# Spectral loop of a convolution, attention and long-filter block: how its PSUM banks, copies and products are arranged

## The chip, the cores and the metric

One core of one Trainium2 chip runs the whole program. The metric is the device time of one execution in microseconds (us). The engines are TensorE (PE, with its weight loads PEld), VectorE (DVE), ScalarE (ACT), GpSimd (POOL) and SyncE (SP), which here issues most DMAs.

## The reference

The input is x of 4 x 56 x 56 x 128 floats. Layer 0 adds a 7 x 7 neighbourhood attention over group-normalised x. Layer 1 sees the image as 3136 tokens of 128 channels. It adds a linear attention, and then the part that matters here: for each of 16 filters k, a causal convolution along the tokens by FFT, followed by a 128 x 128 matrix, once for u and once for u with alternating sign, all summed:

```
U_plus = irfft(rfft(phi)[None, :, :, None] * rfft(u)[:, :, None, :])[:, :sl]
out = einsum('btkd,k,kde->bte', U_plus, s, Mpp) + einsum('btkd,k,kde->bte', U_minus, s, Mpm)
```

The sum over k and d can be taken in the frequency domain: for every frequency there is one complex 128 x 128 matrix, the filter-weighted sum of the M's, which multiplies the transformed tokens.

## The kernel before

The program has three stages. The first 1488.5 us prepare tables, run both attentions and write row transforms of the tokens to a DRAM tile `xd`. The last 154 us (L1036 on) transform columns back and add the result to the output. Between them stands the spectral loop (L881 to L1033), which the change edits. All data are fp32.

The loop runs over N1 = 42 row frequencies m1, with three more iterations to drain (LAG = 3, L1005). Each m1 has N2 = 56 column frequencies m2. One iteration `it` does four things, for different m1 at once:

- `matrices(it, gt, eh)` (L927), for eh = 0 to 7: sixteen matmuls with 32 rows each, four row groups at once, make the complex matrices of all m2 for 16 of the 128 output channels e. They go to two PSUM tiles `pg`, each of two banks: row groups 0 and 1 to the first, 2 and 3 to the second. DVE copies the first tile to `gt` and ACT the second (L941 to L946). `gt` is laid out as m2, e, real/imaginary (L1010), and pool `ps_g` has one buffer for each of the two tiles (L884).
- `token_points(it, ..., s)` (L912), for s = 0 and 1 in the turns eh = 1 and 3: four matmuls make the token transforms of one half into bank `u`; DVE copies real and imaginary parts to `us`, ACT writes the negated imaginary part (L924, L925).
- `product` (L948) for the previous m1 (ap = it - 1): for each m2, two accumulating matmuls with the 16 columns of `us` as weights and `gt[:, m2, :, c]` as moving data, an element every 8 bytes. m2 % 4 picks the column tile, so the result lies on 16 of 32 partitions of a quarter of bank `py`; 16 m2 fill one bank, and `ps_y` has two. Each turn eh does seven m2. `gather` (L961) copies a full `py` to `ys` by four instructions, one for each quarter, alternately on ACT and DVE. `regroup` (L970) sends `ys` to DRAM by four DMAs (`yd`) and fetches it back by two (`yg`).
- `columns(it - 3)` (L984) in the turn eh = 5: two back transforms, each of one matmul of 512 columns into the one bank `z`, copied by ACT (L996), then two DMAs to `zd`.

The trace shows each fp32 matmul as two MATMUL and two LDWEIGHTS records: 28 records are the 14 matmuls of seven m2.

PE's order is that of the text (`manual_schedule`, L1006). For the other engines a scheduler places instructions; in the trace DVE and ACT keep the text's order, and SP's stream in an iteration is `yg`, `xm` (tokens of a later m1, L906), `zd`, `yd`. Tables (`v`, `tok`, `back`) are fetched for six m1 at a time (L890). Semaphores come from the framework: an instruction waits for those that wrote or read the same tile. `evacuate` (L179) is a helper used elsewhere in the program: one copy, ACT and DVE by turns.

Of the kernel before, what the change touches and what calls it, by code (L numbers as in the profile page):

```python
# [10 lines left out]
F32 = mybir.dt.float32  # L11
# [4 lines left out]
P = 128  # L16
B, H, W, C = 4, 56, 56, 128
# [33 lines left out]
NS, BR = 2, H // 2  # L51
N1, N2 = 42, W
NP = N1 * N2
NG = 4
# [66 lines left out]
def hybrid_kernel(  # L121
# [759 lines left out]
    with ExitStack() as ph:  # L881
        tabs = ph.enter_context(tc.tile_pool(name="tabs", bufs=2))
        sp = ph.enter_context(tc.tile_pool(name="sp", bufs=2))
        ps_g = ph.enter_context(tc.tile_pool(name="ps_g", bufs=1, space=bass.MemoryType.PSUM))  # L884
        ps_y = ph.enter_context(tc.tile_pool(name="ps_y", bufs=2, space=bass.MemoryType.PSUM))
        ps_x = ph.enter_context(tc.tile_pool(name="ps_x", bufs=1, space=bass.MemoryType.PSUM))

        chunk = {}

        def tables_of(m1):  # L890

            c0, i = divmod(m1, CH)
            if c0 not in chunk:
                got = []
                for name, src, rows in (
                    ("v", vd, P),
                    ("tok", table["tok"], 2 * N2),
                    ("back", table["back"], 2 * N2),
                ):
                    tl = tabs.tile([rows, CH, 2 * N2], F32, tag=name, name=name)  # L900
                    nc.sync.dma_start(tl, src[:, c0 * CH : (c0 + 1) * CH])
                    got.append(tl)
                chunk[c0] = got
            return [tl[:, i] for tl in chunk[c0]]
# [6 lines left out]

        def token_points(m1, xm, us, s):  # L912

            pu = ps_x.tile([P, B, 2, N2], F32, tag="u", name="pu")
            for b in range(B):
                nc.tensor.matmul(  # L916
                    pu[:, b].rearrange("p c m -> p (c m)"),
                    xm[:, s, b, :],
                    tables_of(m1)[1],
                    start=True,  # L920
                    stop=True,
                )
            at = slice(s * B, (s + 1) * B)
            nc.vector.tensor_copy(us[:, 1:3, at, :], pu.rearrange("p b c m -> p c b m"))  # L924
            nc.scalar.mul(us[:, 0, at, :], pu[:, :, 1, :], -1.0)  # L925

        def matrices(m1, gt, eh):  # L927

            v = tables_of(m1)[0]
            pg = [ps_g.tile([P, 2, 512], F32, tag=f"g{q}", name=f"pg{q}") for q in range(2)]  # L930
            for i in range(4):
                for g in range(NG):
                    rows = slice(32 * g, 32 * (g + 1))
                    nc.tensor.matmul(  # L934
                        pg[g // 2][:, g % 2, 2 * N2 * i : 2 * N2 * (i + 1)],
                        mats[rows, 4 * eh + i, :],
                        v[rows],
                        start=True,
                        stop=True,
                    )  # L940
            for q, copy in enumerate((nc.vector.tensor_copy, nc.scalar.copy)):  # L941
                e0 = 16 * eh + 8 * q
                copy(  # L943
                    gt[:, :, e0 : e0 + 8, :].rearrange("p m (g i) c -> p g m i c", g=2),
                    pg[q][:, :, : 8 * N2].rearrange("p g (i m c) -> p g m i c", i=4, c=2),
                )  # L946

        def product(py, gt, us, m2):  # L948

            j, slot = m2 % NG, m2 // NG % 4  # L950
            for c in range(2):

                nc.tensor.matmul(  # L953
                    py[32 * j : 32 * j + 2 * NSB, slot, :],
                    us[:, 1 - c : 3 - c, :, m2],
                    gt[:, m2, :, c],
                    start=(c == 0),
                    stop=(c == 1),
                )

        def gather(py, ys, q):  # L961

            n = min(4, N2 // NG - 4 * q)
            for j in range(NG):
                rows = slice(32 * j, 32 * j + 2 * NSB)
                (nc.vector.tensor_copy if j % 2 else nc.scalar.copy)(  # L966
                    ys[rows, 4 * q : 4 * q + n], py[rows, :n]
                )

        def regroup(m1, ys):  # L970
# [10 lines left out]
                )  # L981
            return yg

        def columns(m1, yg):  # L984

            zs = sp.tile([2 * N2, NS, B * C], F32, name="zs")
            for s in range(NS):
                pz = ps_x.tile([2 * N2, B * C], F32, tag="z", name="pz")
                nc.tensor.matmul(  # L989
                    pz,  # L990
                    tables_of(m1)[2],
                    yg[:, s * B : (s + 1) * B].rearrange("p k e -> p (k e)"),
                    start=True,
                    stop=True,
                )
                nc.scalar.copy(zs[:, s], pz)  # L996
            for part in range(2):
                nc.sync.dma_start(
                    zd[:, part * N1 + m1].rearrange("w s b e -> w (s b e)"),
                    zs[part * N2 : (part + 1) * N2].rearrange("w s f -> w (s f)"),  # L1000
                )

        xms = {0: load_tokens(0)}
        gts, uss, ygs = {}, {}, {}
        LAG = 3  # L1005
        with tc.manual_schedule(engines={mybir.EngineType.PE}):  # L1006
            for it in range(N1 + LAG):
                ap = it - 1
                if it < N1:
                    gts[it] = sp.tile([P, N2, C, 2], F32, name="gt")  # L1010
                    uss[it] = sp.tile([P, 3, NSB, N2], F32, name="us")
                    if it + 1 < N1:
                        xms[it + 1] = load_tokens(it + 1)
                if 0 <= ap < N1:
                    ys = sp.tile([P, N2 // NG, C], F32, name="ys")
                done = 0
                for eh in range(8):
                    if it < N1:
                        matrices(it, gts[it], eh)
                        if eh in (1, 3):  # L1020
                            token_points(it, xms[it], uss[it], eh // 2)
                    if eh == 5 and 0 <= it - LAG < N1:
                        columns(it - LAG, ygs.pop(it - LAG))
                    if 0 <= ap < N1:
                        for m2 in range(7 * eh, 7 * eh + 7):
                            if m2 % 16 == 0:
                                py = ps_y.tile([P, 4, C], F32, name="py")
                            product(py, gts[ap], uss[ap], m2)
                            if m2 % 16 == 15 or m2 == N2 - 1:
                                gather(py, ys, m2 // 16)  # L1030
                if 0 <= ap < N1:
                    ygs[ap] = regroup(ap, ys)
                xms.pop(it, None), gts.pop(ap, None), uss.pop(ap, None)  # L1033


    with ExitStack() as ph:  # L1036
# [91 lines left out]
```

## Time and profile before

| | us |
|---|---|
| median of three runs | 2741.33 (2734.8 to 2744.59) |
| profiled execution | 2739.52 |
| its span | 2737.7 |
| stages before the loop | 0 to 1488.5, PE busy 997, granted clock 0.65 |
| spectral loop | 1488.5 to 2583.9 (1095.4), PE busy 946, PEld 740, DVE 624, ACT 542, POOL 0, clock 0.98 |
| last stage | 2583.9 to 2737.7, PE busy 126, clock 0.50, DMA share 0.82 |
| copies of `gt`: DVE, ACT | 336 each, 1.091 and 0.906 each |
| copies of `ys`: DVE, ACT | 336 each, 0.69 and 0.57 for 512 elements |

Times of one execution come from a hardware profile. A busy PE is not a PE at its peak, since matmuls are pipelined. Idle time of an engine matters only where it lies on the chain of waits that sets the end: that chain is followed back from the last instruction, at each step to what released it.

### The profile page before, as it was taken

What the parts mean: (1) busy time and instruction counts of PE and PEld (TensorE: products, weight loads), DVE (VectorE), ACT (ScalarE), POOL (GpSimd) and SP (SyncE); (2) the same over time, 40 slices, a digit from 0 to 9 for tenths busy, and PEclk for the clock granted to TensorE, in tenths of its full rate; (3) what the DMA queues carried; (4) which work ended last, traced back from release to release, by engine and by line L of the source; (5) the groups of instructions that cost most, each with busy time, mean ns of one, the idle gap of its engine ahead of it and who ended that gap; (6) DMA issues with size and microseconds to landing.
All of it is one profiled execution on the core that took longest, in us unless ns stands there. A gap on an engine that the chain in (4) does not pass through costs nothing.

```text
span 2737.7 us, 67019 instructions
## 1 busy us (share of the span) xinstructions
PE 2069.0 (76%) x28284; PEld 1419.4 (52%) x28284; DVE 1331.0 (49%) x3228; ACT 1072.3 (39%) x2521; POOL 694.2 (25%) x1227
## 2 busy tenths in 40 slices
PE   3066687666776677776686888888888888888598
PEld 3034456244563445534463767666766666676322
DVE  5244445444454443444432556555555655555232
ACT  0034433344424444244441455555555555555200
POOL 1146734376424664257630000000000000000000
PEclk7565579555885557855585899999999999999755
DMA  6620003300043000420015233333333333333497
GB/s 163 144 88 26 27 1 106 100 26 23 9 113 88 27 19 14 111 66 26 16 44 139 42 81 81 81 81 79 89 78 86 81 86 76 76 80 65 105 229 199
DMA packets 219519, 210.11 MB, mean 77 GB/s; under 512 B 43154, under 2 KB 187250, under 8 KB 218642
## 3 DMA queue, kind: packets, MB, share of 16 engines
q1 hardware_dynamic: 197850, 189.31, 27.9%
q10 hardware_dynamic: 21368, 16.51, 2.3%
q8 instruction: 222, 3.64, 0.5%
q14 instruction: 79, 0.65, 0.1%
HBM read 116.32 MB, written 89.45 MB: 75 GB/s over the span
## 4 chain that ended last, share of the span: by engine, by line
PE 42%; ACT 19%; DVE 18%; DMA 9%; issue 6%; POOL 5%; SPq 1%; ACTq 1%; DVEq 0%; POOLq 0%
ACT st L747 8%; PE pg L934 7%; DVE ys L966 7%; PE py L953 6%; PE sp L723 6%; ACT ys L966 5%; DVE gt L943 5%; PE pt L770 4%; PE bs L543 4%; ACT gt L943 3%; PE po L1059 2%; DMA xd<-xs 2%; DVE st L736 2%; PE pz L989 2%; PE pu L916 2%
## 5 line engine op out<-in xcount | busy, mean ns | idle before, releaser
L758 POOL TENSOR_SCALAR st<-st,rec 96x252 f32<-96x252 f32 (+1 forms) x560 | 484.9, 880 | 370.9 <-DVE rec L756 216.5
L943 DVE COPY gt<-pg 128x896 f32<-128x896 f32 x336 | 366.7, 1091 | 288.4 <-PE pg L934 279.1
L934 PE MATMUL pg<-v,mats 32*128 32x112 f32 x10752 | 398.9, 286 | 103.2 <-DVE gt L943 86.1
L934 PEld LDWEIGHTS pg<-v,mats 32*128 32x128 f32 x10752 | 338.5, 190 | 192.4 <-DVE gt L943 167.1
L747 ACT ACTIVATE st<-st,nmx 96x252 f32<-96x252 f32 (+1 forms) x560 | 270.4, 484 | 351.2 <-DVE nmx L736 351.2
L943 ACT COPY gt<-pg 128x896 f32<-128x896 f32 x336 | 304.4, 906 | 244.7 <-PE pg L934 233.5
L770 PE MATMUL pt<-ident,st 96*126 96x96 f32 (+1 forms) x1120 | 233.8, 360 | 214.6 <-ACT p L774 162.6
L953 PE MATMUL py<-gt,us 128*16 128x128 f32 x9408 | 389.7, 283 | 2.5 <-DVE gt L943 1.6
L770 PEld LDWEIGHTS pt<-ident,st 96*126 96x126 f32 (+1 forms) x1120 | 159.4, 207 | 347.0 <-POOL st L758 252.1
L953 PEld LDWEIGHTS py<-gt,us 128*16 128x16 f32 x9408 | 295.0, 112 | 67.4 <-issue 31.1
L966 DVE COPY ys<-py 16x512 f32<-16x512 f32 (+1 forms) x336 | 209.5, 624 | 160.2 <-ACT ys L966 157.8
L736 DVE CUSTOM_DVE_ANT_0 st<-sp,relb 96x252 f32<-96x252 f32 (+1 forms) x560 | 195.3, 400 | 87.8 <-PE sp L723 87.1
L966 ACT COPY ys<-py 16x512 f32<-16x512 f32 (+1 forms) x336 | 174.6, 520 | 149.2 <-DVE ys L966 141.1
L723 PE MATMUL sp<-kp,qT 32*96 32x252 f32 (+1 forms) x1120 | 162.2, 647 | 3.3 <-DVE xs L185 1.8
L774 DVE COPY p<-pt 126x384 f32<-126x384 f32 (+1 forms) x140 | 74.2, 530 | 160.3 <-PE pt L770 160.3
L594 ACT ACTIVATE hn<-acc,v 128x128 f32<-128x128 f32 (+1 forms) x208 | 88.1, 484 | 153.2 <-POOL v L586 138.9
L1059 PE MATMUL po<-z,onto 84*56 84x512 f32 x224 | 126.0, 1066 | 21.8 <-DMA z<-zd 21.8
L989 PE MATMUL pz<-yg,back 112*112 112x512 f32 x168 | 96.5, 657 | 46.3 <-ACT zs L996 36.2
L785 PE MATMUL po<-p,v_sb 126*32 126x96 f32 (+1 forms) x2240 | 112.6, 349 | 0.8 <-DVE aT L792 0.8
L505 PE MATMUL px<-uin,into 28*84 28x512 f32 x224 | 77.0, 960 | 36.2 <-DVE xs L185 19.7
L747 ACT ACTIVATION_READ_ACCUMULATOR st<-st,nmx 96x1 f32 (+1 forms) x560 | 104.4, 186 | 0.0
L1068 DVE SCALAR_TENSOR_TENSOR tl<-po,hmask,tl 56x512 f32<-56x512 f32 x56 | 42.0, 750 | 124.3 <-PE po L1059 123.7
(162 smaller groups left out, 2221.3 us busy)
## 6 DMA issues: line engine op xcount, KB each, us to landing
xd<-xs SPq DMA_DIRECT2D x112, 168.0 KB
xm<-xd SPq DMA_DIRECT2D x84, 224.0 KB
yd<-ys SPq DMA_DIRECT2D x168, 112.0 KB
yg<-yd SPq DMA_DIRECT2D x84, 224.0 KB
zd<-zs SPq DMA_DIRECT2D x84, 224.0 KB
z<-zd SPq DMA_DIRECT2D x14, 1344.0 KB
v_sb<-vpad SPq DMA_DIRECT2D x224, 63.0 KB
vpad<-vt SPq DMA_DIRECT2D x56, 112.0 KB
```

The lines of the kernel that those rows point to most:

```text
L723: nc.tensor.matmul(sp[h // 2][:nq, h % 2, : 2 * kn], qT[hs, ty, QR * x0 : QR * x0 + nq], kp[hs, y0 : y0 + KR, x0 : x0 + kc], start=True, s ...
L736: nc.vector.tensor_tensor_reduce(st[:nq, h, : 2 * kn], sp[h // 2][:nq, h % 2, : 2 * kn], relb[qc][:, h], -1.0, 3.0e38, ALU.add, ALU.min, n ...
L747: nc.scalar.activation(st[:nq, h, : 2 * kn], st[:nq, h, : 2 * kn], AF.Exp, bias=nmx[:nq, h : h + 1], scale=-1.0, accum_out=ssum[:nq, h : h ...
L758: nc.gpsimd.tensor_scalar(st[:nq, h, : 2 * kn], st[:nq, h, : 2 * kn], rec[:nq, h : h + 1], None, ALU.mult)
L770: nc.tensor.transpose(pt[:kn, h, :nq], st[:nq, h, c * kn : (c + 1) * kn], ident[:nq, :nq])
L785: nc.tensor.matmul(po[hs], v_sb[:kn, c, hs], pc[c][:kn, h, :nq], start=(c == 0), stop=(c == 1),)
L934: nc.tensor.matmul(pg[g // 2][:, g % 2, 2 * N2 * i : 2 * N2 * (i + 1)], mats[rows, 4 * eh + i, :], v[rows], start=True, stop=True,)
L943: copy(gt[:, :, e0 : e0 + 8, :].rearrange("p m (g i) c -> p g m i c", g=2), pg[q][:, :, : 8 * N2].rearrange("p g (i m c) -> p g m i c", i= ...
L953: nc.tensor.matmul(py[32 * j : 32 * j + 2 * NSB, slot, :], us[:, 1 - c : 3 - c, :, m2], gt[:, m2, :, c], start=(c == 0), stop=(c == 1),)
L966: (nc.vector.tensor_copy if j % 2 else nc.scalar.copy)(ys[rows, 4 * q : 4 * q + n], py[rows, :n])
L989: nc.tensor.matmul(pz, tables_of(m1)[2], yg[:, s * B : (s + 1) * B].rearrange("p k e -> p (k e)"), start=True, stop=True,)
L1059: nc.tensor.matmul(po[64 * q : 64 * q + H].rearrange("p b c -> p (b c)"), onto[:, s], zin[q][:, i, s], start=(s == 0), stop=(s == NS - 1),)
```

## The change

Only the spectral loop is edited.

- PSUM: `ps_g` has three buffers of two banks under one tag, so the two `pg` tiles of a turn take two of three in rotation. `py` has one bank (tag y), and one more bank has tag x. Token points and column transforms use bank x for s = 0 and bank y for s = 1.
- `gt` is laid out as e, m2, real/imaginary. Each `pg` tile is copied by two instructions, DVE for its first bank and ACT for its second, each to a contiguous stretch of `gt`. The moving operand of a product, `gt[:, :, m2, c]`, then has an element every 448 bytes.
- `us` has five parts in place of three, of which the last two stay zero; two such tiles are set up once by GpSimd and used by turns. The weights of a product have 32 columns, so that all 128 partitions of `py` are written (half of each quarter's rows are not used), and `evacuate` copies a `py` bank by one instruction.
- The turns eh = 0 to 6 do eight m2 each. The turn eh = 7 has no products; after its matrices it does both token points and then both column transforms. The column results are copied by `evacuate`.
- The two `zd` stores are issued after `regroup`.

```diff
@@ -881,9 +881,16 @@
     with ExitStack() as ph:
         tabs = ph.enter_context(tc.tile_pool(name="tabs", bufs=2))
         sp = ph.enter_context(tc.tile_pool(name="sp", bufs=2))
-        ps_g = ph.enter_context(tc.tile_pool(name="ps_g", bufs=1, space=bass.MemoryType.PSUM))
-        ps_y = ph.enter_context(tc.tile_pool(name="ps_y", bufs=2, space=bass.MemoryType.PSUM))
+        sp1 = ph.enter_context(tc.tile_pool(name="sp1", bufs=1))
+        ps_g = ph.enter_context(tc.tile_pool(name="ps_g", bufs=3, space=bass.MemoryType.PSUM))
+        ps_y = ph.enter_context(tc.tile_pool(name="ps_y", bufs=1, space=bass.MemoryType.PSUM))
         ps_x = ph.enter_context(tc.tile_pool(name="ps_x", bufs=1, space=bass.MemoryType.PSUM))
+
+
+
+        us2 = [sp1.tile([P, 5, NSB, N2], F32, name=f"us{i}") for i in range(2)]
+        for t in us2:
+            nc.gpsimd.memset(t[:, 3:], 0.0)
 
         chunk = {}
 
@@ -911,7 +918,8 @@
 
         def token_points(m1, xm, us, s):
 
-            pu = ps_x.tile([P, B, 2, N2], F32, tag="u", name="pu")
+            pool, tag = ((ps_x, "x"), (ps_y, "y"))[s]
+            pu = pool.tile([P, B, 2, N2], F32, tag=tag, name="pu")
             for b in range(B):
                 nc.tensor.matmul(
                     pu[:, b].rearrange("p c m -> p (c m)"),
@@ -927,7 +935,7 @@
         def matrices(m1, gt, eh):
 
             v = tables_of(m1)[0]
-            pg = [ps_g.tile([P, 2, 512], F32, tag=f"g{q}", name=f"pg{q}") for q in range(2)]
+            pg = [ps_g.tile([P, 2, 512], F32, tag="g", name="pg") for q in range(2)]
             for i in range(4):
                 for g in range(NG):
                     rows = slice(32 * g, 32 * (g + 1))
@@ -938,12 +946,12 @@
                         start=True,
                         stop=True,
                     )
-            for q, copy in enumerate((nc.vector.tensor_copy, nc.scalar.copy)):
-                e0 = 16 * eh + 8 * q
-                copy(
-                    gt[:, :, e0 : e0 + 8, :].rearrange("p m (g i) c -> p g m i c", g=2),
-                    pg[q][:, :, : 8 * N2].rearrange("p g (i m c) -> p g m i c", i=4, c=2),
-                )
+            for q in range(2):
+                for g, copy in enumerate((nc.vector.tensor_copy, nc.scalar.copy)):
+                    e0 = 16 * eh + 8 * q + 4 * g
+                    copy(
+                        gt[:, e0 : e0 + 4].rearrange("p i m c -> p (i m c)"), pg[q][:, g, : 8 * N2]
+                    )
 
         def product(py, gt, us, m2):
 
@@ -951,20 +959,11 @@
             for c in range(2):
 
                 nc.tensor.matmul(
-                    py[32 * j : 32 * j + 2 * NSB, slot, :],
-                    us[:, 1 - c : 3 - c, :, m2],
-                    gt[:, m2, :, c],
+                    py[32 * j : 32 * (j + 1), slot, :],
+                    us.rearrange("p c k m -> p (c k) m")[:, NSB * (1 - c) : NSB * (5 - c), m2],
+                    gt[:, :, m2, c],
                     start=(c == 0),
                     stop=(c == 1),
-                )
-
-        def gather(py, ys, q):
-
-            n = min(4, N2 // NG - 4 * q)
-            for j in range(NG):
-                rows = slice(32 * j, 32 * j + 2 * NSB)
-                (nc.vector.tensor_copy if j % 2 else nc.scalar.copy)(
-                    ys[rows, 4 * q : 4 * q + n], py[rows, :n]
                 )
 
         def regroup(m1, ys):
@@ -981,19 +980,20 @@
                 )
             return yg
 
-        def columns(m1, yg):
-
-            zs = sp.tile([2 * N2, NS, B * C], F32, name="zs")
-            for s in range(NS):
-                pz = ps_x.tile([2 * N2, B * C], F32, tag="z", name="pz")
-                nc.tensor.matmul(
-                    pz,
-                    tables_of(m1)[2],
-                    yg[:, s * B : (s + 1) * B].rearrange("p k e -> p (k e)"),
-                    start=True,
-                    stop=True,
-                )
-                nc.scalar.copy(zs[:, s], pz)
+        def columns(m1, yg, zs, s):
+
+            pool, tag = ((ps_x, "x"), (ps_y, "y"))[s]
+            pz = pool.tile([2 * N2, B * C], F32, tag=tag, name="pz")
+            nc.tensor.matmul(
+                pz,
+                tables_of(m1)[2],
+                yg[:, s * B : (s + 1) * B].rearrange("p k e -> p (k e)"),
+                start=True,
+                stop=True,
+            )
+            evacuate(zs[:, s], pz)
+
+        def store_columns(m1, zs):
             for part in range(2):
                 nc.sync.dma_start(
                     zd[:, part * N1 + m1].rearrange("w s b e -> w (s b e)"),
@@ -1001,36 +1001,43 @@
                 )
 
         xms = {0: load_tokens(0)}
-        gts, uss, ygs = {}, {}, {}
+        gts, ygs = {}, {}
         LAG = 3
         with tc.manual_schedule(engines={mybir.EngineType.PE}):
             for it in range(N1 + LAG):
-                ap = it - 1
+                ap, az = it - 1, it - LAG
                 if it < N1:
-                    gts[it] = sp.tile([P, N2, C, 2], F32, name="gt")
-                    uss[it] = sp.tile([P, 3, NSB, N2], F32, name="us")
+                    gts[it] = sp.tile([P, C, N2, 2], F32, name="gt")
                     if it + 1 < N1:
                         xms[it + 1] = load_tokens(it + 1)
                 if 0 <= ap < N1:
                     ys = sp.tile([P, N2 // NG, C], F32, name="ys")
-                done = 0
+                if 0 <= az < N1:
+                    zs = sp.tile([2 * N2, NS, B * C], F32, name="zs")
                 for eh in range(8):
                     if it < N1:
                         matrices(it, gts[it], eh)
-                        if eh in (1, 3):
-                            token_points(it, xms[it], uss[it], eh // 2)
-                    if eh == 5 and 0 <= it - LAG < N1:
-                        columns(it - LAG, ygs.pop(it - LAG))
-                    if 0 <= ap < N1:
-                        for m2 in range(7 * eh, 7 * eh + 7):
-                            if m2 % 16 == 0:
-                                py = ps_y.tile([P, 4, C], F32, name="py")
-                            product(py, gts[ap], uss[ap], m2)
-                            if m2 % 16 == 15 or m2 == N2 - 1:
-                                gather(py, ys, m2 // 16)
+                    if eh == 7:
+                        for s in range(NS):
+                            if it < N1:
+                                token_points(it, xms[it], us2[it % 2], s)
+                        for s in range(NS):
+                            if 0 <= az < N1:
+                                columns(az, ygs[az], zs, s)
+                    if 0 <= ap < N1 and eh < 7:
+                        if eh % 2 == 0:
+                            py = ps_y.tile([P, 4, C], F32, tag="y", name="py")
+                        for m2 in range(8 * eh, 8 * eh + 8):
+                            product(py, gts[ap], us2[ap % 2], m2)
+                        if eh % 2 or eh == 6:
+                            q, n = eh // 2, 2 if eh == 6 else 4
+                            evacuate(ys[:, 4 * q : 4 * q + n], py[:, :n])
                 if 0 <= ap < N1:
                     ygs[ap] = regroup(ap, ys)
-                xms.pop(it, None), gts.pop(ap, None), uss.pop(ap, None)
+                if 0 <= az < N1:
+                    store_columns(az, zs)
+                    ygs.pop(az)
+                xms.pop(it, None), gts.pop(ap, None)
 
 
     with ExitStack() as ph:
```

## Prediction before the run

> **What bounds the kernel now.** I read the busy table by stages first. The spectral loop fills 1488.5 to 2583.9 us of the span; nothing outside it is edited. From the first products of iteration 1 (1524.05) to the end of iteration 41 (2551.95) there are 41 iterations in 1027.9 us, 25.07 us each. The next view is the busy time of one such iteration, from one DVE copy to the same copy an iteration later (columns: length, then PE, PEld, DVE, ACT, POOL, the granted clock, DMA share, GB/s):
>
> ```profile
> 2014.22:2039.39 25.17, 22.18 (x500) 17.35 (x500) 14.86 (x19) 12.88 (x22) 0.00 (x0) 1.00 0.37 88
> ```
>
> PE looks full, yet DVE and ACT have ten us to spare, and DMA is at 0.37. So I asked for the chain of waits over the same iteration, as shares by line and then piece by piece in order of time:
>
> ```profile
> by line: PE pg L934 18.1%; DVE ys L966 17.2%; PE py L953 15.4%; ACT ys L966 13.6%; DVE gt L943 13.0%; ACT gt L943 10.7%; PE pz L989 4.4%; issue 4.4%; PE pu L916 4.2%; ACT zs L996 3.9%; ACTq L966 0.1%
> ```
> ```profile
> 2019.26 0.58 ACT ys L966
> 2019.85 0.02 issue
> 2019.87 0.69 DVE ys L966
> 2020.56 0.02 issue
> 2020.59 0.59 ACT ys L966
> 2021.17 0.02 issue
> 2021.20 0.70 DVE ys L966
> 2021.89 0.03 issue
> 2021.93 1.09 DVE gt L943
> ```
>
> PE holds under half of the chain. The four copies of one `py` tile (16 partitions each) run strictly one after the other, 2.6 us, and the `gt` copy queued behind them on DVE keeps the only pair of `pg` banks closed. The groups by shape and the wait view (instruction, whom it waited for, us, times, longest) give durations and PE's idle time:
>
> ```profile
> L943 DVE COPY gt<-pg 128x896 f32<-128x896 f32 x9 | 9.8, 1091 | 6.6 <-PE pg L934 6.5
> L943 ACT COPY gt<-pg 128x896 f32<-128x896 f32 x9 | 8.2, 906 | 5.3 <-PE pg L934 5.2
> L966 DVE COPY ys<-py 16x512 f32<-16x512 f32 x6 | 4.1, 690 | 3.3 <-ACT ys L966 3.3
> L966 ACT COPY ys<-py 16x512 f32<-16x512 f32 x6 | 3.4, 573 | 2.4 <-DVE ys L966 2.3
> L924 DVE COPY us<-pu 128x448 f32<-128x448 f32 x2 | 1.2, 618 | 0.0
> ```
> ```profile
> PEld pg L934 <- DVE gt L943: 3.8, 6, 1.8
> PEld pz L989 <- ACT zs L996: 1.7, 1, 1.7
> ```
>
> **What the Trainium skill says.** "PSUM — Partial Sum Buffer", PSUM bank collisions raise a hardware error: two engines must be kept off one bank and quadrant, while different quadrants may be read together. The trace agrees that something serialises, but by whole bank: the four `ys` copies lie in four quadrants and still alternate, while the `gt` copies from two banks start 0.06 us apart. "TensorE: Matmul & The Clock Gate", LDWEIGHTS: a load costs columns/1.2 ns. Single records agree: the 16-column loads of the four column tiles start 13 ns apart. "TensorEngine Tiling (Array Packing)", Key Properties: changing the tiling mode drains the array; the fixed part of a group, worked out below, agrees. "SBUF — State Buffer", The DMA port swizzle, on cachelines: a line is 16 bytes, and each access that crosses to a new line pays. The weights of the products, read 224 bytes apart, keep 13 ns for 16 columns and show no such payment; for a moving operand no row of before shows it.
>
> **PE's own prices.** Starts of groups in the chain: matrices 1.09 us, products 1.09 (28 records), token points 1.07, a column transform about 1.04. Products in the drain: 12 records take 0.67 and 28 take 1.16, so a round of four costs 0.49/4 = 0.122 us and the fixed part of a group is 1.09 - 7 x 0.122 = 0.24.
>
> **The change, part by part.**
> *Four gathers become one copy.* A copy of 512 elements costs 0.69 (DVE) or 0.57 (ACT) whatever its partitions, so 2.6 us of alternation becomes one of these. Three long and one short per iteration go.
> *Three bank pairs.* A group takes two of three, so the next group's second pair is the last one's first. The `gt` work per group becomes two 448-element copies on each engine: DVE 2 x 0.62 (the `us` row has this size); ACT, from 0.573 and 0.906 us at 512 and 896 elements, 0.87 ns each, so 2 x 0.52. That is 1.24 and 1.04 for 1.09 and 0.91: more work, in a period of over 2.3 us, hence hidden. The first pair is free 0.7 us after its matrices; the products in front of the next matrices cover that. Without that cover (iteration 0) it is paid. The contiguous write itself saves nothing[...].
> *Weights of 32 columns, eight products, seven groups.* Per iteration the 224 product records stay, as 7 groups of 8 rounds. The unknown is the round. Below: 0.107 us, the 128 columns themselves[...]. Above: four loads, each 13 ns longer and none hidden, 0.122 + 0.053 = 0.175. I take 0.130, since each load follows the start of its own tile's preceding matmul and only its own lengthening shows. A group is 0.24 + 8 x 0.130 = 1.28.
> *Moving operand.* `gt` read 448 bytes apart instead of 8: taken at nothing, because the weights at 224 bytes and fp32 moving data are both read at 0.83 ns an element. The other bound is half rate, rival A. A gain is excluded: an 8-byte step already streams near the column rate.
> *One `py` bank for two.* Its copy starts some 1.37 us after the product group starts (behind two `gt` copies) and ends at 2.06; the next products start at 2.37. Hidden by the 1.09 of matrices, with 0.3 us of slack; if the copy came behind the next matrices' copies, 1.9 us three times would show, but the trace keeps program order on both engines.
> *Transforms in one turn.* From the end T of the last matrices, PE does both token points (to T+1.9). The first column transform needs bank x: DVE is in `gt` copies to T+1.3, `us` to 1.92, ACT's `us` (0.36, it waits for DVE as now) to 2.3, so it starts at 2.4, a new stall of 0.7. Then 0.85 and 1.04 us for the two transforms: next matrices at T+4.27. The second's bank y is free at 3.0, in time. Its copy ends near T+5.0; the products that need the bank start at T+5.3. The new `us` is ready at 3.0, also before T+5.3.
> *DMAs.* Same count and bytes. `xm` now comes free at the iteration's end and is wanted two iterations later. On SP, the two `zd` stores go behind four `yd`, and two `yg` that wait for them some 6 us (2022.37 to 2028.42 now); behind `zd` stand the next `xm`, needed over 20 us later, and `yg` is needed two iterations on. All hidden by the LAG of 3. Two GpSimd memsets at the start are needed only in iteration 1: nothing.
>
> **Sum.** Seven turns of 1.09 + 1.28 = 2.37 make 16.6; the last matrices 1.16 and the tail 4.27 make 5.4. An iteration is 22.0, that is 3.1 less than 25.07; times 41 = 127 us. Iteration 0 now pays about 3.25 us for each group at half clock; with a spare pair about 2.8, and later transforms: 5 us in all. The drain at the end keeps its DMA waits. The profiled execution took 2739.5 us (span 2737.7), so 2739.5 - 132 = 2607. The median of the runs shown, 2741.3, is 2 us higher, inside their spread; I keep 2607. What is late next is PE itself, then the tail's wait for `us`.
>
> **Rivals.**
> *A, slower: the strided moving operand.* 128 elements 448 bytes apart, four column tiles streaming at once, one new line per element where two shared one. At half rate each round grows by 0.107: 56 x 0.107 = 6.0 us, an iteration of 28.0, +120 - 5: 2854. It decides against the change from 3.1/56 = 0.055 us a round, half of the full penalty. For: the skill's line on cachelines, and four streams at once where loads come one by one. Against: the unharmed strided weights, and the DVE copy at L348, 336 elements from PSUM 168 bytes apart in 0.504 us[...].
> *B, smaller gain: the wider loads bind.* Rounds at 0.175: +2.5, an iteration of 24.5; 0.57 x 41 + 5 = 28 less: 2711. For: loads of the four tiles go one at a time, 4 x 27 = 107 ns, the whole round. Against: they start while the preceding matmul streams.
> *C, no change: the copies of one tile's two banks serialise across engines, or the copy order slips,* and a new wait replaces the gathers': about 2740. Against: waits now go by bank, and the DVE and ACT copies of `gt` already run together.
>
> **Numbers.** Forecast 0.58 (its own range 2560 to 2655: rounds of 0.115 to 0.145, waits of 0.4 us either way), B 0.20, C 0.04, A 0.18. The lower end is the round of 0.107: 4.4 x 41 + 5 = 184 less, 2555. The upper end takes in B and C, 2740; A is left out. A measurement of this kernel tells about 0.3% from no change: faster by more than that 0.78, within it 0.04, slower by more 0.18.
>
> **What would show it.** Right: no `ys`-behind-`ys` waits, `gt` copies of 0.62 and 0.52 us, product groups 1.28 us apart from the next matrices, PE idle only at the column transforms, an iteration of 22. Wrong: product matmuls well over 0.28 us each or groups over 1.8 (A), loads with groups of 1.6 (B), ACT `gt` waiting for DVE `gt` (C).

## The result and the profile after

The changed kernel takes 2822.18 us (median of four runs, 2815.72 to 2827.99) where the kernel before takes 2739.98 (four runs, 2734.80 to 2744.59): a ratio of 1.03, with a 95% interval of 1.027 to 1.033. The forecast of 2607 was 215 us too low; rival A, given a chance of 0.18, had said 2854. The profiled execution took 2820.85 us, its span 2819.1.

The stages show where the time went (busy table, columns as in the prediction):

```profile
0.00:1488.50 1488.50, 995.96 (x7060) 647.43 (x7060) 663.72 (x2415) 531.14 (x1681) 696.17 (x1227) 0.65 0.22 61
1488.50:2668.00 1179.50, 1143.67 (x21000) 845.08 (x21000) 514.71 (x883) 461.79 (x882) 1.63 (x2) 0.98 0.33 74
2668.00:2819.10 151.10, 125.74 (x224) 32.85 (x224) 41.99 (x56) 0.00 (x0) 0.00 (x0) 0.50 0.82 213
```

The loop alone has grown, by 84 us, and now PE is busy for 97% of it (86% before). DVE and ACT work less than before. The chain of waits over one iteration says the same by line, and then piece by piece:

```profile
by line: PE py L961 52.1%; PE pg L942 33.0%; PE pz L987 8.9%; ACT gt L952 3.9%; DVE gt L952 2.3%; ACT us L933 1.3%; issue 0.6%; ACTq L933 0.1%
...
2060.80 1.09 PE pg L942 x32
2061.89 2.07 PE py L961 x29
2063.95 1.09 PE pg L942 x32
2065.04 2.02 PE py L961 x28
```

Copies of `ys`, 31% of the chain before, are gone, and copies of `gt` fell from 24% to 6%. Products rose from 15% to 52%: a group of eight takes 2.0 us, where 1.28 was forecast. The matrices are at their 1.09. The groups by shape, of the same iteration, name the kind of instruction:

```profile
L961 PE MATMUL py<-gt,us 128*32 128x128 f32 x224 | 14.7, 408 | 0.0
L952 DVE COPY gt<-pg 128x448 f32<-128x448 f32 x16 | 9.2, 620 | 11.3 <-PE pg L942 11.3
L952 ACT COPY gt<-pg 128x448 f32<-128x448 f32 x16 | 8.5, 536 | 14.5 <-DVE gt L952 14.5
```

No engine keeps the products waiting: idle time before them (the last column) is 0.0. The copies of `gt` take 0.620 and 0.536 us for the forecast 0.62 and 0.52. (ACT's 14.5 us behind DVE are taken up below.) Next the duration of the product records over the whole loop, as lowest/median/highest ns, in the kernel before and then in the changed one:

```profile
L953 PEld LDWEIGHTS py<-gt,us x9408: 106/108/145, 1522.2 to 2563.0; 128*16 128x16 f32 x196
L953 PE MATMUL py<-gt,us x9408: 273/278/415, 1522.2 to 2563.1; 128*16 128x128 f32 x196
```
```profile
L961 PEld LDWEIGHTS py<-gt,us x9408: 134/141/178, 1521.7 to 2648.5; 128*32 128x32 f32 x196
L961 PE MATMUL py<-gt,us x9408: 393/404/462, 1521.7 to 2648.8; 128*32 128x128 f32 x196
```

Count and size of the matmuls are the same, and their median went from 278 to 404 ns. Loads went from 108 to 141. Both signs that the prediction named for rival A are there: records well over 0.28 us, and groups over 1.8. Two edits touch these records: the step of the moving operand (rival A) and the 32 weight columns (rival B). The experiments separate them.

An iteration is measured below as the median distance between the first token-point matmuls of neighbouring iterations, 41 of them: 25.18 us before, 27.19 after. Times 41 the difference is 82 us, as much as the whole loss.

### The profile page after: what moved, and what is told of

The parts are those of the page before. It is cut to its first block, busy times and chain, and to the rows that moved or that the text cites. A ratio compares the mean times of both kernels' runs of the same rounds, so it can differ in the third digit from the quotient of the medians.

```text
span 2819.1 us, 67241 instructions
## 1 busy us (share of the span) xinstructions
PE 2265.4 (80%) x28284; PEld 1525.4 (54%) x28284; DVE 1220.4 (43%) x3354; ACT 992.9 (35%) x2563; POOL 697.8 (25%) x1229
## 4 chain that ended last, share of the span: by engine, by line
PE 62%; ACT 12%; DMA 9%; DVE 8%; POOL 4%; issue 4%; SPq 1%; ACTq 1%; DVEq 0%; POOLq 0%
PE py L961 21%; PE pg L942 13%; ACT st L747 8%; PE sp L723 5%; PE pt L770 4%; PE bs L543 3%; PE pz L987 3%; DMA xd<-xs 3%; PE po L1066 2%; DVE st L736 2%; ACT gt L952 2%; PE bs L824 2%; DMA z<-zd 1%; ACT p L774 1%; POOL st L758 1%
## 5 line engine op out<-in xcount | busy, mean ns | idle before, releaser
L961 PE MATMUL py<-gt,us 128*32 128x128 f32 x9408 | 617.9, 409 | 3.3 <-ACT ys L183 1.4
L952 DVE COPY gt<-pg 128x448 f32<-128x448 f32 x672 | 388.3, 619 | 479.4 <-PE pg L942 475.1
L952 ACT COPY gt<-pg 128x448 f32<-128x448 f32 x672 | 357.9, 535 | 618.1 <-DVE gt L952 618.1
L961 PEld LDWEIGHTS py<-gt,us 128*32 128x32 f32 x9408 | 403.7, 145 | 107.6 <-ACT ys L183 2.4
L987 PE MATMUL pz<-yg,back 112*112 112x512 f32 x168 | 85.9, 635 | 18.0 <-ACT us L933 10.6
L1066 PEld LDWEIGHTS po<-z,onto 84*56 84x56 f32 x224 | 32.9, 206 | 114.6 <-issue 98.0
L543 PE MATMUL bs<-mu,ut 128*128 128x128 f32 (+1 forms) x528 | 80.6, 319 | 12.4 <-DVE ut L185 6.2
L756 DVE RECIPROCAL rec<-ssum 96x2 f32<-96x2 f32 x280 | 44.7, 160 | 103.6 <-ACT st L747 89.9
```

The costliest lines, as they stand in the source:

```text
L543: nc.tensor.matmul(pt[:r, o : o + C], lhs[:, t0 : t0 + 2 * r - 1 : 2], rhs, start=(i == 0), stop=(i == len(terms) - 1),)
L952: copy(gt[:, e0 : e0 + 4].rearrange("p i m c -> p (i m c)"), pg[q][:, g, : 8 * N2])
L961: nc.tensor.matmul(py[32 * j : 32 * (j + 1), slot, :], us.rearrange("p c k m -> p (c k) m")[:, NSB * (1 - c) : NSB * (5 - c), m2], gt[:, : ...
L987: nc.tensor.matmul(pz, tables_of(m1)[2], yg[:, s * B : (s + 1) * B].rearrange("p k e -> p (k e)"), start=True, stop=True,)
L1066: nc.tensor.matmul(po[64 * q : 64 * q + H].rearrange("p b c -> p (b c)"), onto[:, s], zin[q][:, i, s], start=(s == 0), stop=(s == NS - 1),)
```

## The experiments

The theory after the result is that the 448-byte step of `gt` costs some 0.1 us a round, that is, for four product records, one in each column tile. The rivals: the wider loads; or the new arrangement of copies and banks.

**The step undone in the changed kernel.** `gt` gets its old layout again; everything else of the change stays.

```diff
-                        gt[:, e0 : e0 + 4].rearrange("p i m c -> p (i m c)"), pg[q][:, g, : 8 * N2]
+                        gt[:, :, e0 : e0 + 4].rearrange("p a i k c -> p i a (k c)"),
+                        pg[q][:, g, : 8 * N2].rearrange("p (i a f) -> p i a f", i=4, a=N2 // 1),
...
-                    gt[:, :, m2, c],
+                    gt[:, m2 // 1, :, m2 % 1, c],
...
-                    gts[it] = sp.tile([P, C, N2, 2], F32, name="gt")
+                    gts[it] = sp.tile([P, N2 // 1, C, 1, 2], F32, name="gt")
```

> The changed kernel with gt laid out as before (m2, e, real/imaginary), so that a product's moving operand again has an element every 8 bytes; everything else as changed. Theory S (the step of the moving operand halves its rate): product records fall from 404 ns back to about 285, a group from 2.05 us to about 1.28, the iteration from 27.2 us to about 22, the whole to about 2610 us. Theory L (the 32-column weight loads set the round): records stay near 400 ns, the iteration near 27, the whole near 2820.

2612.11 us, a ratio to before of 0.9525 (0.9511 to 0.9539); an iteration takes 22.09. Its product records:

```profile
L962 PEld LDWEIGHTS py<-gt,us x9408: 134/140/183, 1518.4 to 2439.6; 128*32 128x32 f32 x196
L962 PE MATMUL py<-gt,us x9408: 273/281/430, 1518.4 to 2439.7; 128*32 128x128 f32 x196
```

The loads are as long as in the changed kernel, the matmuls as short as before the change. So the wider loads are not what lengthens the matmuls. The step is, and it costs 210 us of 2822.

**The step alone, in the kernel before.**

```diff
-                    gt[:, :, e0 : e0 + 8, :].rearrange("p m (g i) c -> p g m i c", g=2),
-                    pg[q][:, :, : 8 * N2].rearrange("p g (i m c) -> p g m i c", i=4, c=2),
+                    gt[:, e0 : e0 + 8].rearrange("p (g i) m c -> p g (i m c)", g=2),
+                    pg[q][:, :, : 8 * N2],
...
-                    gt[:, m2, :, c],
+                    gt[:, :, m2, c],
```

> The kernel before with gt laid out as e, m2, real/imaginary alone, so that the moving operand has an element every 448 bytes; 16-column weights, gathers, banks and order as before. Theory S: product records go from 278 to about 390 ns; 56 rounds are 0.1 us longer each, 5.8 us an iteration, of which up to 3 may fall into PE's waits: 28 to 31 us an iteration, 2860 to 2985 us in all. Theory L: nothing moves, 25.1 us an iteration, 2740 us.

2934.68 us, 1.0705 (1.0689 to 1.0721), an iteration of 29.94, that is 4.8 more. The matmuls grow as in the changed kernel, with weights of 16 columns:

```profile
L953 PE MATMUL py<-gt,us x9408: 382/396/439, 1523.6 to 2762.8; 128*16 128x128 f32 x196
```

**The 32 weight columns alone, in the kernel before.** The two fixed `us` tiles of five parts come with it.

```diff
-                    py[32 * j : 32 * j + 2 * NSB, slot, :],
-                    us[:, 1 - c : 3 - c, :, m2],
+                    py[32 * j : 32 * (j + 1), slot, :],
+                    us.rearrange("p c k m -> p (c k) m")[:, NSB * (1 - c) : NSB * (5 - c), m2],
```

> The kernel before with products' weights of 32 columns alone (us with two zero parts, two such tiles by turns); gathers still copy 16 rows of each quarter. Theory S: the loads take 13 ns more each and stay mostly hidden, at most 0.7 us an iteration: 2740 to 2770 us. Theory L: product records go to about 400 ns and the iteration to 28 us or more, 2860 us and up.

2750.54 us, 1.0029 (1.002 to 1.0039); an iteration takes 25.41, 0.23 more than before. The loads are 31 ns longer, where 13 were expected (the reason is found below, in the weights' own step), and nearly all of that lies beside matmuls. Rival B is small: 9 us.

**The step at 16 bytes.** As the first experiment, with two m2 side by side in `gt` (`[P, N2 // 2, C, 2, 2]`, read as `gt[:, m2 // 2, :, m2 % 2, c]`).

> The changed kernel with gt laid out as m2 pair, e, m2 of the pair, real/imaginary: the moving operand has an element every 16 bytes. If the price is that of one element to a 16-byte line (S16), the product records stay near 400 ns and the whole near 2820 us. If it comes with larger steps only (Sfar), they fall to about 285 ns and the whole to about 2610 us. Theory L: near 2820 us as well, told apart by the 8-byte run.

One execution: 2829.07 us, beside 2741.52 for the kernel before. An iteration takes 27.34.

```profile
L962 PE MATMUL py<-gt,us x9408: 402/414/455, 1523.5 to 2656.2; 128*32 128x128 f32 x196
```

The full price is there at 16 bytes: 448 bytes cost no more. The Trainium skill, "SBUF — State Buffer", The DMA port swizzle, on cachelines, says that a line of 16 bytes needs two hits for full speed; with a step of 8 bytes each line serves two elements, with 16 only one, and the runs agree. The same passage gives four fp32 as the step that is free; that is these 16 bytes, and the measurement decides against it.

**The step at 4 bytes.** Real and imaginary parts in separate rows of `gt` (`[P, 2 * N2, C]`), each moving operand contiguous.

```diff
-                        gt[:, e0 : e0 + 4].rearrange("p i m c -> p (i m c)"), pg[q][:, g, : 8 * N2]
+                        gt[:, :, e0 : e0 + 4].rearrange("p f i -> p i f"),
+                        pg[q][:, g, : 8 * N2].rearrange("p (i f) -> p i f", i=4),
...
-                    gt[:, :, m2, c],
+                    gt[:, 2 * m2 + c],
```

> The changed kernel with gt laid out as m2, real/imaginary, e: the moving operand is contiguous, an element every 4 bytes; the copies write single elements 512 bytes apart. If two elements to a 16-byte line are enough, product records stay at 281 ns and the whole at 2612 us (plus what scattered writes cost DVE and ACT, hidden up to about 0.2 us a turn). If more elements to a line still help, the records fall below 275 ns and the whole by up to 10 us.

2813.02 us, 1.0264 (1.0249 to 1.028): the 2612 was missed by 200, while the matmuls did what was expected of them. Their records even fall from 281 to 273 ns, so that a step of 8 bytes still costs some 8 ns of a record. The rows show where the time went:

```profile
L962 PE MATMUL py<-gt,us x9408: 272/273/433, 1526.7 to 2639.6; 128*32 128x128 f32 x196
L952 DVE COPY gt<-pg x672: 889/932/1015, 1495.5 to 2625.1; 128x448 f32<-128x448 f32 x168
L952 ACT COPY gt<-pg x672: 905/923/963, 1496.5 to 2626.1; 128x448 f32<-128x448 f32 x168
```

The copies now write single elements 512 bytes apart, and take 0.93 and 0.92 us for the changed kernel's 0.62 and 0.535. The waits of PE and its loads (1700 to 2300 us, some 22 iterations) carry it:

```profile
PEld pg L942 <- ACT gt L952: 79.1, 156, 0.7
...
PE pg L942 <- ACT gt L952: 51.4, 156, 0.6
```

Both rows tell of the same 156 stops, once for the loads and once for the matmuls behind them, so they are not to be added. An iteration takes 27.04, 4.95 more than with 8 bytes. By the starts of the groups, its eight groups of matrices take 14.5 us in place of 9.5 and the turn with the transforms 0.5 more, while the products take 0.6 less. The scattered access has moved from the reader to the writers.

**Pairs far apart.** Two neighbouring e of one frequency side by side in 8 bytes, the next pair 896 bytes on. If the sharing of a line counts, this is free; if distance counts, it costs as much as the change.

```diff
-                        gt[:, e0 : e0 + 4].rearrange("p i m c -> p (i m c)"), pg[q][:, g, : 8 * N2]
+                        gt[:, e0 // 2 : e0 // 2 + 2],
+                        pg[q][:, g, : 8 * N2].rearrange("p (j i f) -> p j f i", j=2, i=2),
...
-                    gt[:, :, m2, c],
+                    gt[:, :, 2 * m2 + c],
```

> The changed kernel with gt laid out as e pair, m2, real/imaginary, e of the pair: two elements of the moving operand lie side by side in 8 bytes, and the pairs 896 bytes apart; the copies read their banks 448 bytes apart and write one contiguous stretch. Theory H (what counts is that two elements share a line, wherever the next line is): product records near 281 ns and the whole near 2612 us. Theory D (distance between lines costs too): records of 340 ns or more, 2700 us or more.

2608.81 us, 0.9524 (0.9507 to 0.9541), an iteration of 21.91.

```profile
L962 PE MATMUL py<-gt,us x9408: 269/273/435, 1521.5 to 2434.1; 128*32 128x128 f32 x196
L952 DVE COPY gt<-pg x672: 614/620/629, 1494.9 to 2419.5; 128x448 f32<-128x448 f32 x168
L952 ACT COPY gt<-pg x672: 532/532/538, 1495.6 to 2420.2; 128x448 f32<-128x448 f32 x168
```

No payment, at twice the changed kernel's distance. What counts is whether two neighbours lie together. Banks, order and the division of the copies are those of the changed kernel, so the third rival goes too: only the place of the elements in `gt` differs. The copies, which write whole stretches and read PSUM 448 bytes apart, pay nothing either.

**One stream instead of four.** In the first experiment's kernel, the column transform alone (no column tiles) reads `yg` in steps of 512 bytes; its PSUM output stays contiguous and `zs` is written back into place by the copy.

```diff
-                pz,
+                pz.rearrange("p (e k) -> p e k", k=B),
                 tables_of(m1)[2],
-                yg[:, s * B : (s + 1) * B].rearrange("p k e -> p (k e)"),
+                yg[:, s * B : (s + 1) * B].rearrange("p k e -> p e k"),
...
-            evacuate(zs[:, s], pz)
+            evacuate(zs[:, s].rearrange("p (k e) -> p e k", k=B), pz.rearrange("p (e k) -> p e k", k=B))
```

> The changed kernel with the 8-byte step for gt (as e1_step8), and in the column transform alone the moving operand yg read in another order, an element every 512 bytes; one matmul streams there, without column tiles. The output order in its bank changes with it and the copy puts it back. Theory P (the price belongs to each moving stream): the column records go from 624 to about 1050 ns, 1.7 us an iteration more than e1_step8, about 2680 us. Theory Q (the price comes from four streams at once): the records stay near 624 ns and the whole near 2612 us.

2684.57 us, 0.9792 (0.9777 to 0.9807), an iteration of 23.81. The transform's rows with the old step (first experiment) and with 512 bytes:

```profile
L988 PE MATMUL pz<-yg,back x168: 592/625/1163, 1577.1 to 2453.6; 112*112 112x512 f32 x168
L183 ACT COPY zs<-pz x42: 586/586/587, 1578.3 to 2453.0; 112x512 f32<-112x512 f32 x42
L185 DVE COPY zs<-pz x42: 690/692/693, 1579.1 to 2454.6; 112x512 f32<-112x512 f32 x42
```
```profile
L988 PE MATMUL pz<-yg,back x168: 1047/1047/1167, 1581.5 to 2524.6; 112*112 112x512 f32 x168
L183 ACT COPY zs<-pz x42: 1024/1024/1025, 1583.5 to 2524.0; 112x512 f32<-112x512 f32 x42
L185 DVE COPY zs<-pz x42: 1023/1045/1048, 1585.3 to 2525.8; 112x512 f32<-112x512 f32 x42
```

Between the shortest records this is (1047 - 592)/512 = 0.89 ns an element, with one stream; in the products it is (393 - 273)/128 = 0.94. So four streams at once are not needed for it. Four records an iteration, 0.455 us each, make 1.8, beside 1.72 us by which the iteration grew. The copies pay here too, as scattered writers.

**Two bank pairs for three.** In the first experiment's kernel, `ps_g` has `bufs=2`.

> As e1_step8, with two buffers in place of three for the matrices' bank pairs: each group of matrices must wait for both copies of the one before. ACT's first copy starts behind DVE's (0.66 us), so its second ends 1.8 us after the matrices, while the products cover 1.25: about 0.5 us a turn and 3.5 us an iteration, about 2755 us. If the third pair is worth nothing: 2612 us.

2730.75 us, 0.997 (0.9963 to 0.9978), an iteration of 25.05. Its wait view, 1700 to 2300 us:

```profile
PEld pg L942 <- ACT gt L952: 72.5, 333, 0.5
```

The same row with three pairs:

```profile
PEld pg L942 <- ACT gt L952: 10.7, 58, 0.4
```

With copies split between engines the third pair is worth 3.0 us an iteration. The loads' wait for ACT's copies is 3.0 us in each of the 24 iterations of this stretch, and 0.4 in each of 27 with three pairs, so it carries most of the difference.

**One engine for a tile.** A version put together from the findings: the first experiment's kernel, with each `pg` tile copied whole by one engine as in the kernel before, two pairs, and two banks each for `pu` and for `py` with `pz`. Three edits at once, so that their shares aren't told apart.

```diff
-        ps_g = ph.enter_context(tc.tile_pool(name="ps_g", bufs=3, space=bass.MemoryType.PSUM))
-        ps_y = ph.enter_context(tc.tile_pool(name="ps_y", bufs=1, space=bass.MemoryType.PSUM))
-        ps_x = ph.enter_context(tc.tile_pool(name="ps_x", bufs=1, space=bass.MemoryType.PSUM))
+        ps_g = ph.enter_context(tc.tile_pool(name="ps_g", bufs=2, space=bass.MemoryType.PSUM))
+        ps_y = ph.enter_context(tc.tile_pool(name="ps_y", bufs=2, space=bass.MemoryType.PSUM))
+        ps_x = ph.enter_context(tc.tile_pool(name="ps_x", bufs=2, space=bass.MemoryType.PSUM))
...
+            for q, copy in enumerate((nc.vector.tensor_copy, nc.scalar.copy)):
+                e0 = 16 * eh + 8 * q
+                copy(
+                    gt[:, :, e0 : e0 + 8].rearrange("p m (g i) k c -> p g m i (k c)", g=2),
+                    pg[q][:, :, : 8 * N2].rearrange("p g (i m c) -> p g m i c", i=4, c=2),
+                )
...
```

> As e1_step8, with each matrices' tile copied whole by one engine (DVE the first, ACT the second, 896 elements), two pairs of banks for them, two banks for py and the column transforms, two for the token points. Copies end 1.1 us after the matrices, under the products' 1.25, ACT no longer waits for DVE, and the first column transform no longer waits for us: 0.2 us a turn and 0.5 us at the end of an iteration less, about 20.4 us an iteration and 2545 us in all. If a wait takes their place: 2612 us or more.

2574.2 us, 0.9397 (0.9381 to 0.9412): ahead of both kernels, but 29 us behind what was expected. Its busy table for one iteration, and a row of its wait view (1700 to 2300 us):

```profile
2047.74:2068.96 21.22, 21.15 (x504) 17.36 (x501) 11.77 (x13) 9.63 (x13) 0.00 (x0) 1.00 0.39 89
```
```profile
PEld pg L941 <- DVE gt L950: 47.5, 191, 0.4
```

Each group of matrices takes 1.09 us again, and the turn with the transforms is 0.56 shorter. But from the products to the next matrices it is 1.25 us, more than the 1.19 of the first experiment, because the loads of the matrices now wait for DVE's whole copy of 1.09 us.

**Dense weights.** On top of it, `us` is laid out as m2, part, filter, so that the 32 columns of a load are contiguous.

```diff
-        us2 = [sp1.tile([P, 5, NSB, N2], F32, name=f"us{i}") for i in range(2)]
+        us2 = [sp1.tile([P, N2, 5 * NSB], F32, name=f"us{i}") for i in range(2)]
...
-                    us.rearrange("p c k m -> p (c k) m")[:, NSB * (1 - c) : NSB * (5 - c), m2],
+                    us[:, m2, NSB * (1 - c) : NSB * (5 - c)],
```

> As e9_best, with us laid out as m2, part, row, so that the 32 weights of a product lie side by side in place of 224 bytes apart; DVE and ACT write us in runs of four. Theory W (strided weights pay the same price as strided moving data: the 16 more columns added 28 ns to a load, 1.75 ns each, where side by side they would add 13): loads fall from 134 to about 106 ns, as those of 32 dense columns at L785, and the products' rounds from 0.124 to about 0.115 us: 0.5 us an iteration less, about 2555 us. If strided weights pay nothing: loads stay at 134 ns, 2574 us.

2573.68 us, 0.9391 (0.9377 to 0.9405), an iteration of 21.21, exactly as without, where 2555 was expected. The loads, a stretch of its PE and load timelines (start, us), and its wait view:

```profile
L961 PEld LDWEIGHTS py<-gt,us x9408: 106/108/171, 1522.8 to 2400.0; 128*32 128x32 f32 x196
```
```profile
2046.79 1.17 PE L961 MATMUL py<-gt,us 128*32 128x128 f32 x32
```
```profile
2048.04 0.98 PEld L942 LDWEIGHTS pg<-v,mats 32*128 32x128 f32 x32 [0.36 <-DVE gt L951]
```
```profile
PEld pg L942 <- DVE gt L951: 72.0, 196, 1.3
```

The loads fell from 134 to 106 ns. But the product group, busy for 1.17 us, is still followed by the next matrices only 1.25 us after its start: they wait for DVE to copy `gt` out of one of the two pairs. That wait was there before and has grown from 47.5 to 72.0 us. The loads gained what was expected, and the wait took it.

**Dense weights with three pairs.** The same, with `ps_g` at three buffers again and one bank each for x and y as in the changed kernel.

> As e11_best_dense_weights, but with three pairs of banks for the matrices, and bank x and bank y shared again by py, token points and column transforms (the arrangement of the change). If in e11 the shorter loads gained nothing because the next matrices then waited for DVE's copy of 1.09 us (a wait of 0.36 us before the loads), that wait goes: 1.17 us from products to matrices in place of 1.25, and 0.7 us less an iteration, while the column transform waits for us again, 0.5 us more: about 2568 us. If another thing holds the products at 1.25 us, about 2590 us.

2580.36 us, 0.9419 (0.9405 to 0.9434), an iteration of 21.29: no gain, and the main expectation missed. Its chain:

```profile
2044.07 1.09 PE pu L924 x8
...
2045.19 0.64 DVE us L933
...
2045.90 0.36 ACT us L934
...
2046.31 2.00 PE pz L988 x4
2048.32 1.09 PE pg L943 x32
2049.41 1.09 PE py L962 x32
2050.50 1.29 PE pg L943 x32
```

Products stand at 1.09 now, but every other group of matrices takes 1.23 to 1.29, and with one bank each for x and y the column transforms again wait for `us` (1.15 us from 2045.16 to 2046.31). What holds the long groups can be read from the trace. The last one shown (2050.50 in the chain, which counts from the end of the group before) starts at 2050.43; DVE's copy of the group before began at 2049.50 and takes 1.09 us, until 2050.59; the next loads for that pair of banks begin at 2050.64. The shorter products no longer cover a whole copy by DVE. No run took this wait away.

## Why the prediction was wrong

**The step that failed** is "Moving operand. `gt` read 448 bytes apart instead of 8: taken at nothing, because the weights at 224 bytes and fp32 moving data are both read at 0.83 ns an element". The runs put 2.03 us in place of 1.19 from the start of a product group to the next matrices, so (2.03 - 1.19)/8 = 0.105 us a round. Rival A had said 0.107, with the right mechanism. A's 2854 was 32 us high because its 6.0 us an iteration were put on top of the forecast whole: 7 x 0.84 = 5.9 were lost, but the eight groups of matrices of an iteration, 9.5 us with the step undone, take 8.7 in the changed kernel, since the longer products cover the matrices' wait. That gives 0.8 back. From 22.09 to 27.19 it is 5.1.

**Why it was taken at nothing: the evidence was misread.** The strided weights were called unharmed because loads of the four column tiles start 13 ns apart. A distance of starts is not a price: records of 108 ns that start 13 ns apart overlap. The duration of a record was the thing to read, and two rows of the kernel before together gave the hint: 16 strided columns take at least 106 ns (L953 above), and so do 32 contiguous ones, in the attention:

```profile
L785 PEld LDWEIGHTS po<-p,v_sb x2240: 106/155/178, 193.3 to 1357.1; 126*32 126x32 f32 x150, 98*32 98x32 f32 x37
L989 PEld LDWEIGHTS pz<-yg,back x168: 172/176/312, 1584.7 to 2580.6; 112*112 112x112 f32 x168
```

With the same stride, 16 more columns cost (134 - 106)/16 = 1.75 ns each, and made contiguous the 32 fall back to 106. The price in the Trainium skill, "TensorE: Matmul & The Clock Gate", LDWEIGHTS, of columns/1.2 ns (0.83 a column) gives the rise for contiguous columns only: 32 and 112 of them took 106 and 172 ns, (172 - 106)/80 = 0.83. The fp32 moving data that were called as a witness do stream at that rate, (592 - 273)/(512 - 128) = 0.83 in the first experiment, but with steps of 4 and 8 bytes. The last witness, a DVE copy of 336 elements from PSUM 168 bytes apart in 0.504 us, spoke of another reader and another memory. The pairs experiment confirms that reading PSUM 448 bytes apart is free to DVE and ACT; it says nothing of what they would pay in SBUF.

**The sum held otherwise.** With the step undone the iteration is 22.09 for a forecast of 22.0, and the time 2612.11 for 2607. By its terms:

- The gathers went as forecast. A copy of 512 elements takes 0.586 or 0.692 us, and no `ys` copy stands on the chain of the changed kernel's iteration.
- A product group was forecast at 1.28 and is 1.19 with the step undone: the wider loads were priced too high, as rival B's small effect shows (9 us alone). With dense weights it is 1.09, so the wide strided loads still cost some 0.1 us a group.
- The matrices were forecast at 1.09 and take 1.19 there on average, from 1.09 to 1.33. Here rival C's mechanism is real. DVE and ACT copy two banks of one tile, and ACT waits for DVE: its two copies start when DVE's first has ended. So the first pair is free not 0.7 us after its matrices but 1.3 (they end at 2046.15 in the chain, and ACT's first copy at 2046.92 + 1.07/2 = 2047.46 below). The next matrices have begun at 2047.28 and want it for their second tile: the trace has these loads at 2047.52.

These are lines of the DVE and ACT timelines and of the chain of the kernel with the step undone:

```profile
2046.26 1.16 DVE L952 COPY gt<-pg 128x448 f32<-128x448 f32 x2 [0.46 <-PE pg L942]
```
```profile
2046.92 1.07 ACT L952 COPY gt<-pg 128x448 f32<-128x448 f32 x2 [2.13 <-DVE gt L952]
```
```profile
2046.15 1.20 PE py L962 x32
2047.35 1.32 PE pg L942 x32
2048.67 1.18 PE py L962 x31
2049.85 1.12 PE pg L942 x32
```

The prediction had read the old trace as "by whole bank". It goes by tile: before, each `pg` tile had a single reader. In the changed kernel ACT waits 618 us for DVE over the loop. PE's matmuls wait only 8 us for ACT's copies and the loads of the matrices 79.5, under the cover of the long products: the matrices are at 1.09 there. So the sign that was named for C is there, but it is not what made this kernel slow. With one engine for a tile, ACT and DVE start together and both wait for PE alone.

- The errors of these terms, -0.09 and +0.10 in each turn, nearly cancel, and that is luck; a sum that comes out is no proof of each term.
- The tail was right. With the step undone the last matrices end at 2040.82, the column transforms start 2.24 us later (2.4 forecast), and the next matrices 4.24 later (4.27 forecast).
- The third pair was right in kind, and worth 3.0 us an iteration. The DMAs stayed hidden: the chain of the iteration names none.

## What to carry to other kernels

Before a layout is turned to make a copy contiguous, follow every reader and writer of the tile: in fp32, here, two elements that are accessed one after the other want to lie within the same 16 bytes, and a layout in pairs served the copy and the product alike. Take an operand's price from the duration of records in the same role, dense and strided side by side, and not from distances of starts or from another engine's rows. When a faster step leaves the time unchanged, as the dense weights did, look at what the next group waits for.

## What the runs showed of the hardware that was not expected

- An fp32 moving operand costs about 0.9 ns more an element as soon as neighbours don't share 16 bytes: steps of 16, 448 and 512 bytes alike. A record of 128 elements took 273 ns at 4 bytes and in pairs 896 bytes apart, 281 at 8 bytes, 414 at 16 and 404 at 448.
- Weights pay as well: a load of 32 columns 224 bytes apart took 134 ns, and 106 with the columns side by side.
- Scattered single writes to SBUF cost the vector and scalar engines as well: 512 elements took 1.045 us for 0.692 on DVE and 1.024 for 0.586 on ACT. Writes of 8 bytes together took 0.621 and 0.549 for 448 elements, where contiguous ones took 0.621 and 0.535.
- Reads of PSUM 448 bytes apart took 0.620 and 0.532 us for 448 elements: nothing more.
